# Graph layer on one core: eight segments instead of six, zero writes in equal steps, a staged tail, and a bias that ScalarE copies into PSUM

## Chip, cores and metric

The kernel runs on one core of one Trainium2 chip. The metric is the device time of one execution in microseconds, as the median of the runs. Five engines work side by side, each in the order of its own instructions: TensorE (PE, with its weight loads as PEld), VectorE (DVE), ScalarE (ACT), GpSimd (POOL) and SyncE (SP). SP, ACT and POOL issue the DMA transfers, and each of these queues is in order too.

## The reference

A SchNet-like graph layer with a residual. There are 12,500 nodes of 128 features and 412,500 edges, which come sorted by `dst`.

```python
def ssp(x):
    return jax.nn.softplus(x) - LOG2
hn = jnp.maximum(_layernorm(x, axis=-1), 0.0)
h = hn @ W_in2f                                               # 12500 x 128
Wij = ssp(edge_attr_20 @ W_f1 + b_f1) @ W_f2 + b_f2           # 412500 x 128
Wij = Wij * edge_weight[:, None]
agg = jax.ops.segment_sum(h[dst] * Wij, src, num_segments=12500)
out = x + ssp(agg @ W_o1 + b_o1) @ W_o2 + b_o2
```

So each edge reads the row of its `dst`, which lies close to the row of the edge before it, makes a message, and adds it to the row of its `src`, which lies anywhere.

## The kernel before

**Edges.** They are cut into 806 chunks of 512 edges (four tiles of 128), four chunks to a group, 202 groups. `step(k)` writes out by hand, for all engines, what is issued around chunk `k`, each piece of it for another chunk so that the pieces overlap: `hidden`, `hidden_log` and `hidden_end` make the softplus of the first layer for two chunks at a time (tiles `z`, `a`, `r`); `blocks`, `rank` and `rank_end` work out a free slot for every edge (`free` in PSUM, read by L660); `window`, `picked` and `value` make the two factors of the message; `message` multiplies them on DVE (L741, tile `o`, four buffers of two chunks) and issues four indirect DMAs on POOL (L745), one for each tile, which scatter the 128 rows into a table in HBM.

**The bias b_f2.** `value` (L723) opens the accumulation of a PSUM bank with a product of three rows of ones and three bf16 parts of the bias (L726), and adds the four products with `W_f2` to it (L730). `picked` (L709) makes the selected `h` rows in another bank (L714) and ACT copies them, scaled by the edge weight, into `hg` (L719). Both kinds of bank share the tag `v` with three buffers. The order in a step is product of chunk k (DVE), `value` of k+1, `picked` of k+1.

**Segments.** `SEGS` (L23) cuts the groups into six segments, each with its own slot table. A table gives every block of 128 nodes `T` tiles of 128 slots, and one more where the sorted `dst` of the segment bring the self loops; `T` follows from the segment's mean count and four standard deviations. When the last chunk of a segment is scattered, `Collect` reads the table back in units of up to six tiles: `load` (L783, SP queue, five buffers), `compare` (L794, DVE, a one-hot matrix of the place in the block), `add` (L807, two passes of TensorE for each tile). Four blocks, a quad, share one PSUM bank with a single buffer; when the quad is complete, `keep` adds it into `agg` (L824, DVE; the first segment's is an ACT copy, L822). Units are spread over later steps by a planner (L917 to L932) that gives each segment the smallest even rate of tiles with which all of it is done by step 812. In a step, `compare` comes after the message, `add` (one unit late) after the rank, and `rank_end` after `add`.

**Zero writes.** Slots that may stay empty must hold zeros. `clear` (L500) lists the DMA writes of a segment, each up to `ZN * ZR` = 32 slot rows for each of up to 128 half blocks, and L904 to L915 put them at steps: the first segment's before chunk 108, the second's in chunks 128 to 246, all others' in chunks 128 to 470. SP issues them at the start of a step. The first scatter past a given chunk of the first segment waits for that segment's writes.

**Tail.** After the loop the last segment is collected unit by unit (L970 to L977), and for each complete quad `finish` (L375) loads `x` (ACT queue), multiplies by `W_o1` (L389), does the softplus in four ACT instructions and one DVE sum (L366 to L373), multiplies by `W_o2` (L398), adds `b_o2` (L401) and the result (L402) to `x` on DVE, and stores (L403, SP queue). If a slot count was exceeded anywhere, a flag makes the kernel repeat the work in a plain loop (`anyway`).

Of the kernel before, what the change touches and what calls it, by code (L numbers as in the profile page):

```python
# [9 lines left out]
F32 = mybir.dt.float32  # L10
# [3 lines left out]
AF = mybir.ActivationFunctionType  # L14
ALU = mybir.AluOpType
PSUM = bass.MemoryType.PSUM

P = 128
TG = 16
CH = 512  # L20
NCHUNK = TG * P // CH
QT = CH // P
SEGS = (64, 56, 32, 24, 14, 12)  # L23
RW = P + 1
VIEWS = 16
BG = 8
ZR = 8
ZN = 4
WR = 32
UT = 6  # L30
BIG = float(1 << 11)
# [9 lines left out]
def gnn_kernel(  # L41
# [20 lines left out]
    nc = tc.nc  # L62
    N, D = x.shape
    NG, _, RBF, _ = f_t.shape
# [7 lines left out]
    const = ctx.enter_context(tc.tile_pool(name="const", bufs=1))  # L72

    NBLK = NTILE
# [52 lines left out]
    NQ = ceil_div(N, QN)  # L127
# [15 lines left out]
    state = ctx.enter_context(tc.tile_pool(name="state", bufs=1))  # L143
# [13 lines left out]
    for c0 in range(0, NC, P):  # L157
        n = min(P, NC - c0)
# [14 lines left out]
    for q in range(NQ):  # L173
        cs = slice(quad_of.index(q), quad_of.index(q) + quad_of.count(q))
# [29 lines left out]
    def spread(t, n):  # L204
        return t[:, None, :].to_broadcast([t.shape[0], n, P])
# [14 lines left out]
    flag = const.tile([1, 1], I32, name="flag")  # L220
# [9 lines left out]
    ones_b = const.tile([P, P], BF16, name="ones_b")  # L230
# [8 lines left out]
    nbf1 = const.tile([P, 1], F32, name="nbf1")  # L239
    nc.vector.tensor_scalar(nbf1, bf1, -1.0, None, op0=ALU.mult)  # L240

    bf2_p = const.tile([3, P], BF16, name="bf2_p")
    left = const.tile([1, P], F32, name="bf2_left")
    with tc.tile_pool(name="bias_ps", bufs=1, space=PSUM) as bias_ps:
        b12 = bias_ps.tile([1, P], F32, name="b12")
        nc.tensor.matmul(b12, bf1, wf2, start=True, stop=True)
        nc.vector.tensor_add(left, b12, bf2[0:1, :])
    for k in range(3):
        part = const.tile([1, P], BF16, name=f"bf2_{k}")
        nc.vector.tensor_copy(part, left)  # L250
# [117 lines left out]

    def softplus_end(a, r):

        nc.scalar.activation(a, a, AF.Exp, scale=-1.0)
        nc.scalar.activation(a, a, AF.Ln, bias=half, scale=0.5)
        nc.vector.tensor_add(r, r, a)  # L373

    def finish(t0, n, sT, edge, quad, psum):  # L375

        n0 = t0 * P
        full = min(n, N // P - t0)
        rest = N - n0 - full * P if full < n else 0
        xo = quad.tile([P, QT, P], F32, name="xo")  # L380
        pieces = []
        if full:
            pieces.append((P, slice(0, full), slice(n0, n0 + full * P)))
        if rest:
            pieces.append((rest, slice(full, n), slice(n0 + full * P, N)))
        for p, cs, rows in pieces:
            nc.scalar.dma_start(xo[:p, cs, :], x[rows, :].rearrange("(c p) f -> p c f", p=p))
        z = psum.tile([P, 2, CH], F32, name="z_out", tag="z")[:, 0, :n * P]
        nc.tensor.matmul(z, wo1, sT, start=True, stop=True)  # L389
        a = edge.tile([P, QT, P], F32, name="a_out")  # L390
        r = edge.tile([P, QT, P], F32, name="r_out")
        a_n = a[:, :n, :].rearrange("p c f -> p (c f)")
        r_n = r[:, :n, :].rearrange("p c f -> p (c f)")
        softplus_parts(a_n, r_n, z, bo1)
        softplus_end(a_n, r_n)
        v = psum.tile([P, QT, P], F32, name="v_out", tag="v", bufs=3)
        for i in range(n):
            nc.tensor.matmul(v[:, i, :], r[:, i, :], wo2, start=True, stop=True)  # L398
        for p, cs, rows in pieces:
            xi = xo[:p, cs, :]  # L400
            nc.vector.tensor_add(xi, xi, spread(bo2[:p, :], xi.shape[1]))  # L401
            nc.vector.tensor_add(xi, xi, v[:p, cs, :])  # L402
            nc.sync.dma_start(out[rows, :].rearrange("(c p) f -> p c f", p=p), xi)  # L403


    def anyway(edge, quad, psum):
        none = edge.tile([P, SUMT // parts * P], F32, name="none", bufs=1)
        nc.vector.memset(none, 0.0)
        rows = sums[:, :].rearrange("(p a c) f -> a p (c f)", p=P, a=parts)
# [3 lines left out]
        with tc.For_i(0, NG, 1) as g:  # L413
            f = edge.tile([P, CH], F32, name="f")
# [12 lines left out]
            a = edge.tile([P, NCHUNK, CH], F32, name="a")  # L427
            r = edge.tile([P, NCHUNK, CH], F32, name="r")
# [45 lines left out]
        for t0 in range(0, NTILE, QT):  # L474
            n = min(QT, NTILE - t0)
            o = quad.tile([P, QT, P], F32, name="s_out")
            nc.sync.dma_start(o[:, :n, :], sums[t0 * P:(t0 + n) * P, :].rearrange("(c p) f -> p c f", p=P))
            tps = psum.tile([P, QT, P], F32, name="t_out", tag="nodes")
            for i in range(n):
                nc.tensor.transpose(tps[:, i, :], o[:, i, :], ident)  # L480
            sT = quad.tile([P, QT, P], F32, name="sT")
            nc.scalar.activation(sT[:, :n, :], tps[:, :n, :], AF.Copy)
            finish(t0, n, sT[:, :n, :].rearrange("p c f -> p (c f)"), edge, quad, psum)


    with tc.tile_pool(name="edge", bufs=2) as edge, tc.tile_pool(
# [4 lines left out]
        kept = {}  # L491
# [40 lines left out]
        class Group:  # L532
# [170 lines left out]
            def window(self, c):  # L703

                at = quad.tile([WP, CH], BF16, name="at")
                nc.vector.tensor_tensor(at, self.rel[:, c, :], prow, op=ALU.is_equal)  # L706
                self.pick = at

            def picked(self, c, at):  # L709

                ps = psum.tile([P, QT, P], F32, name="picked", tag="v", bufs=3)
                near = self.near.pop(c)
                for i in range(QT):
                    nc.tensor.matmul(ps[:, i, :], at[:, i * P:(i + 1) * P], near,  # L714
                                     start=True, stop=True)
                hg = quad.tile([P, QT, P], F32, name="hg", bufs=2)
                for i in range(QT):
                    j = c * QT + i
                    nc.scalar.activation(hg[:, i, :], ps[:, i, :], AF.Copy,  # L719
                                         scale=self.rcut[:, j:j + 1])  # L720
                return hg

            def value(self, c):  # L723

                v = psum.tile([P, QT, P], F32, name="v", bufs=3)
                nc.tensor.matmul(v.rearrange("p t f -> p (t f)"), ones_b[:3, :], spread(bf2_p, QT),  # L726
                                 start=True, stop=False, skip_group_check=True)
                r = self.pair[c // 2 * 2][:, c % 2, :]
                for i in range(QT):
                    nc.tensor.matmul(v[:, i, :], r[:, i * P:(i + 1) * P], wf2,  # L730
                                     start=False, stop=True, skip_group_check=True)
                return v

            def message(self, c, v, hg):

# [95 lines left out]
        def of(k):  # L831
            return groups[k // NCHUNK], k % NCHUNK

        hgs, ats, vs = {}, {}, {}

        summed = []

        def step(k, units=()):
# [24 lines left out]
            if has(k + 2):  # L863
                g, c = of(k + 2)
                g.window(c)
                ats[k + 2] = g.pick
# [34 lines left out]
        collects = [Collect(seg) for seg in segs]  # L901
        AHEAD = 3

        seg = segs[0]  # L904
        todo = clear(seg)
        for i, d in enumerate(todo):
            zeros.setdefault(i * (seg.cleared - 20) // len(todo), []).append((seg, d))
        todo = clear(segs[1])
        for i, d in enumerate(todo):
            zeros.setdefault(seg.cleared + i * (seg.c1 - 10 - seg.cleared) // len(todo),  # L910
                             []).append((segs[1], d))
        todo = [(seg, d) for seg in segs[2:] for d in clear(seg)]
        for i, d in enumerate(todo):
            zeros.setdefault(segs[0].cleared + i * (segs[2].c0 - 10 - segs[0].cleared)
                             // len(todo), []).append(d)  # L915
# [33 lines left out]
        with tc.manual_schedule():  # L949
# [17 lines left out]
                step(k, now)  # L967
                next(aside, None)
            summed[0].add(summed[1])
        last = collects[-1]  # L970
        for u in range(len(last.units)):
            last.load(u)
            last.compare(u)
            last.add(u)
            for done in last.kept:
                finish(*done, edge, quad, psum)
            last.kept = []  # L977
        worst = state.tile([1, 1], F32, name="worst")
        nc.vector.tensor_reduce(worst, bad, axis=mybir.AxisListType.X, op=ALU.max)
        nc.vector.tensor_copy(flag, worst)  # L980

    missed = nc.values_load(flag[0:1, 0:1], min_val=0, max_val=P)
    with tc.If(missed > 0):
# [53 lines left out]
```

## Time and profile before

| | us |
|---|---|
| median of 3 runs | 4383.54 (4381.74 to 4402.45) |
| the profiled execution | 4396.31 |
| its span, first to last instruction | 4394.5 |
| first scatter starts | 85.1 |
| last scatter starts | 4220.6 |
| first compare of the last segment | 4234.8 |

The mean granted TensorE clock is 0.855. Over the span it goes from 0.64 to 0.72 in the stretches up to 1400 us, where hardly anything is collected, to 0.90 to 0.95 after it. The memory traffic is 829 MB, 189 GB/s on average. The zero writes are 164 DMAs of up to 2,064 KB, the table reads 829 of 193.5 to 387 KB.

In the groups of instructions a row gives the line, engine, operation, what is written from what, the count, busy time, mean ns of one, and the engine's idle time just before with what ended it. In the stretches a row gives start and end, length, the engine's busy time with its count, granted clock, DMA share and GB/s. A row of a timeline gives start, duration, engine, line and operation, and in brackets how long the engine was idle before and what released it.

### The profile page before, as it was taken

How to read it: one execution, taken by the hardware profiler on the slowest of the kernel's cores; microseconds unless marked ns; L12 is line 12 of the kernel's file. 1: busy time of each engine (PE TensorE's matmuls, PEld its weight loads, DVE VectorE, ACT ScalarE, POOL GpSimd, SP SyncE). 2: the span in 40 equal slices, each digit the busy share in tenths (PEclk: the TensorE clock that was granted, in tenths of full speed). 3: DMA queues.
4: the chain of work that ended last, by engine and by line, in shares of the span. 5: the costliest groups of instructions: out<-in, count | busy, mean ns of one | idle time of the engine just before them, and what ended most of it. 6: DMA issues, size and time to landing. Idle time of an engine off the chain costs nothing.

```text
span 4394.5 us, 72656 instructions
## 1 busy us (share of the span) xinstructions
PE 3607.4 (82%) x22558; PEld 2618.3 (60%) x22558; DVE 3140.1 (71%) x6637; ACT 2332.5 (53%) x4685; POOL 3114.6 (71%) x3288
## 2 busy tenths in 40 slices
PE   3767776777777888888788889999899998989877
PEld 2544444444444666666566567777677776767666
DVE  5766666566555776767667678787888878888766
ACT  3655555555555555555555555555555555545424
POOL 2777777677777777777777777777777777777620
PEclk9776666667666898899998899999999999999999
DMA  5766547888765666765876566666666766766666
GB/s 139 192 178 230 174 128 197 223 223 230 183 208 135 177 178 183 238 193 166 257 197 174 150 179 187 194 195 185 189 188 183 199 191 185 193 188 191 172 180 192
DMA packets 498071, 829.10 MB, mean 189 GB/s; under 512 B 170680, under 2 KB 288300, under 8 KB 497676
## 3 DMA queue, kind: packets, MB, share of 16 engines
q1 hardware_dynamic: 378950, 602.34, 51.2%
q0 software_dynamic: 103168, 213.15, 14.7%
q10 hardware_dynamic: 15558, 8.89, 0.7%
q8 instruction: 182, 2.98, 0.3%
q14 instruction: 213, 1.74, 0.1%
HBM read 425.03 MB, written 398.98 MB: 188 GB/s over the span
## 4 chain that ended last, share of the span: by engine, by line


## 5 line engine op out<-in xcount | busy, mean ns | idle before, releaser
L745 POOL DMA_INDIRECT slots<-o,slot x3224 | 3108.4, 964 | 1106.3 <-issue 803.6
L719 ACT ACTIVATE hg<-picked,rcut 128x128 f32<-128x128 f32 x3224 | 920.8, 369 | 1372.0 <-PE picked L714 1323.5
L807 PEld LDWEIGHTS acc<-to,m 128*128 128x128 f32 x8312 | 1078.7, 205 | 353.8 <-issue 187.7
L807 PE MATMUL acc<-to,m 128*128 128x128 f32 x8312 | 1154.6, 294 | 92.3 <-DVE agg L824 47.3
L730 PEld LDWEIGHTS v<-wf,r 128*128 128x128 f32 x6448 | 918.1, 220 | 303.7 <-issue 303.7
L730 PE MATMUL v<-wf,r 128*128 128x128 f32 x6448 | 1088.2, 320 | 0.0
L616 PE MATMUL z<-f,wf 20*128 20x512 f32 x1612 | 524.2, 726 | 217.5 <-DVE r L631 190.9
L794 DVE TENSOR_TENSOR to<-count_ps,m 128x768 f32<-128x768 f32 (+3 forms) x829 | 657.9, 812 | 51.8 <-PE acc L807 27.7
L619 ACT ACTIVATE a<-z,bf 128x1024 f32<-128x1024 f32 x403 | 449.1, 1114 | 426.7 <-PE z L616 426.7
L660 DVE TENSOR_REDUCE top<-free 128x4 f32<-128x392 f32 x806 | 447.2, 555 | 211.7 <-PE free L655 210.4
L631 DVE SCALAR_TENSOR_TENSOR r<-z,nbf,a 128x1024 f32<-128x1024 f32 x403 | 514.6, 1277 | 94.2 <-ACT a L625 92.5
L741 DVE TENSOR_TENSOR o<-v,hg 128x512 f32<-128x512 f32 x806 | 547.2, 679 | 2.8 <-ACT hg L719 2.1
L739 DVE COPY o<-place 128x8 f32<-128x8 f32 x403 | 80.4, 200 | 650.9 <-DMA slots<-o,slot 650.6
L714 PE MATMUL picked<-near,at 96*128 96x128 bf16 x3224 | 356.4, 240 | 218.0 <-DVE o L741 215.7
L625 ACT ACTIVATE a<-a,half 128x1024 f32<-128x1024 f32 x403 | 468.4, 1162 | 0.0
L636 DVE TENSOR_TENSOR inb<-count_ps,blk 128x392 f16<-128x392 f32 x806 | 445.7, 553 | 0.0
L726 PE MATMUL v<-bf_p,ones_b 3*128 3x512 bf16 x806 | 350.1, 434 | 104.1 <-DVE o L741 93.9
L620 ACT ACTIVATE a<-a 128x1024 f32<-128x1024 f32 x403 | 425.9, 1057 | 12.8
L714 PEld LDWEIGHTS <-at 96*128 96x128 bf16 x3224 | 275.7, 109 | 256.2 <-DVE o L741 224.6
L616 PEld LDWEIGHTS z<-f,wf 20*128 20x128 f32 x1612 | 142.4, 206 | 388.9 <-issue 186.3
L687 PE MATMUL free<-inb,rest_of 128*128 128x392 f16 x806 | 303.1, 376 | 55.0 <-DVE top L660 53.8
L706 DVE TENSOR_TENSOR at<-rel,prow 96x512 bf16<-96x512 bf16 x806 | 331.1, 411 | 0.0
(107 smaller groups left out, 1416.2 us busy)
## 6 DMA issues: line engine op xcount, KB each, us to landing
m<-slots SPq DMA_DIRECT2D x371, 387.0 KB
rel<-rel_d SPq DMA_DIRECT2D x202, 384.0 KB
m<-slots SPq DMA_DIRECT2D x172, 322.5 KB
m<-slots SPq DMA_DIRECT2D x212, 258.0 KB
slots<-o,slot POOLq DMA_INDIRECT x3224
slots<-zero SPq DMA_DIRECT2D x24, 2064.0 KB
f<-in_f_t SPq DMA_DIRECT2D x404, 80.0 KB
slots<-zero SPq DMA_DIRECT2D x22, 1032.0 KB
```

The lines of the kernel that those rows point to most:

```text
L616: nc.tensor.matmul(z[:, k, :], wf1[rows, :], self.f[rows, :], start=True, stop=True)
L619: nc.scalar.activation(a, z, AF.Abs, bias=bf1)
L625: nc.scalar.activation(a, a, AF.Ln, bias=half, scale=0.5)
L631: nc.vector.scalar_tensor_tensor(r, z, nbf1, a, op0=ALU.max, op1=ALU.add)
L660: nc.vector.tensor_reduce(self.top[:, c * QT:(c + 1) * QT], free_v, axis=mybir.AxisListType.X, op=ALU.max)
L714: nc.tensor.matmul(ps[:, i, :], at[:, i * P:(i + 1) * P], near, start=True, stop=True)
L719: nc.scalar.activation(hg[:, i, :], ps[:, i, :], AF.Copy, scale=self.rcut[:, j:j + 1])
L730: nc.tensor.matmul(v[:, i, :], r[:, i * P:(i + 1) * P], wf2, start=False, stop=True, skip_group_check=True)
L741: nc.vector.tensor_mul(o[:, :, :P], v, hg)
L745: put = nc.gpsimd.indirect_dma_start(out=views[j % VIEWS], out_offset=bass.IndirectOffsetOnAxis(ap=self.slot[:, j:j + 1], axis=0), in_=o[: ...
L794: nc.vector.tensor_tensor(to[:, :n, :], count_ps[:, None, :].to_broadcast([P, n, P]), self.m[u][:, :n, P:].to_broadcast([P, n, P]), op=ALU ...
L807: nc.tensor.matmul(self.acc[b // QT][:, i, :], m[:, j, :P], to[:, j, :], start=t == 0, stop=t == self.seg.tiles(b) - 1)
```

## The change

- `SEGS` becomes eight segments of 68, 52, 30, 14, 14, 8, 8 and 8 groups.
- `ZN` becomes 1, so that a zero write covers 8 slot rows of a half block instead of 32. All segments' writes go through one rule that gives each segment a due step and spreads the writes evenly up to it.
- `value` splits: `bias` fills the bank two chunks ahead, for chunks 0 and 1 with the product as before, for all others with an ACT copy of `bf12` (the bias on all partitions); `value` adds the four products to it. `picked` splits into `pick` (the four products, now one accumulation group of the bank) and `picked` (the four ACT copies). ACT's order in a step is the bias of k+2, then the copies of k+1.
- `bf12` is made in the preamble by a product with 128 columns instead of one.
- The tail comes into the hand-written order. `finish` becomes a generator of six stages, which are issued for different quads around each `add`: load of `x` (now SP), `b_o2` on POOL, first product and softplus on ACT, sum on DVE, second product, result and store. `xo` has six buffers; `a_out` and `r_out` share the loop's tiles. The flag is worked out ahead of the tail.

```diff
-SEGS = (64, 56, 32, 24, 14, 12)
+SEGS = (68, 52, 30, 14, 14, 8, 8, 8)
...
-ZN = 4
+ZN = 1
...
-        b12 = bias_ps.tile([1, P], F32, name="b12")
-        nc.tensor.matmul(b12, bf1, wf2, start=True, stop=True)
-        nc.vector.tensor_add(left, b12, bf2[0:1, :])
+        b12 = bias_ps.tile([P, P], F32, name="b12")
+        nc.tensor.matmul(b12, bf1.to_broadcast([P, P]), wf2, start=True, stop=True)
+        nc.vector.tensor_add(bf12, b12, bf2)
+    nc.vector.tensor_copy(left, bf12[0:1, :])
...
-    def finish(t0, n, sT, edge, quad, psum):
+    def finish(t0, n, sT, quad, psum):
...
-        xo = quad.tile([P, QT, P], F32, name="xo")
+        xo = quad.tile([P, QT, P], F32, name="xo", bufs=6)
...
-            nc.scalar.dma_start(xo[:p, cs, :], x[rows, :].rearrange("(c p) f -> p c f", p=p))
+            nc.sync.dma_start(xo[:p, cs, :], x[rows, :].rearrange("(c p) f -> p c f", p=p))
+        yield
+        for p, cs, rows in pieces:
+            xi = xo[:p, cs, :]
+            nc.gpsimd.tensor_add(xi, xi, spread(bo2[:p, :], xi.shape[1]))
+        yield
...
         softplus_parts(a_n, r_n, z, bo1)
-        softplus_end(a_n, r_n)
+        softplus_logs(a_n)
+        yield
+        nc.vector.tensor_add(r_n, r_n, a_n)
+        yield
...
+            nc.tensor.matmul(v[:, i, :], r_n[:, i * P:(i + 1) * P], wo2, start=True, stop=True)
+        yield
         for p, cs, rows in pieces:
             xi = xo[:p, cs, :]
-            nc.vector.tensor_add(xi, xi, spread(bo2[:p, :], xi.shape[1]))
             nc.vector.tensor_add(xi, xi, v[:p, cs, :])
...
+            def bias(self, c):
+
+
+                v = psum.tile([P, QT, P], F32, name="v", bufs=3)
+                if self.g * NCHUNK + c < 2:
+                    nc.tensor.matmul(v.rearrange("p t f -> p (t f)"), ones_b[:3, :],
+                                     spread(bf2_p, QT), start=True, stop=False,
+                                     skip_group_check=True)
+                else:
+                    nc.scalar.activation(v, spread(bf12, QT), AF.Copy)
+                return v
...
             if has(k + 1):
                 g, c = of(k + 1)
-                vs[k + 1] = g.value(c)
+                vs[k + 1] = g.value(c, bs.pop(k + 1))
+                ps = psum.tile([P, QT, P], F32, name="picked", tag="v", bufs=3)
+                g.pick(c, ats.pop(k + 1), ps)
+            if has(k + 2):
+
+                bs[k + 2] = of(k + 2)[0].bias(of(k + 2)[1])
             if has(k + 1):
-                g, c = of(k + 1)
-                hgs[k + 1] = g.picked(c, ats.pop(k + 1))
+                hgs[k + 1] = g.picked(c, ps)
...
+        clears = [(seg, d) for seg in segs for d in clear(seg)]
+        due = [seg.cleared - 20 if seg is segs[0] else seg.c0 - 10 for seg in segs]
+        todo = [sum(seg is s for s, _ in clears) for seg in segs]
+        t0, i = 0, 0
+        while i < len(segs):
+
+            j = max(range(i, len(segs)), key=lambda j: sum(todo[i:j + 1]) / (due[j] - t0))
+            n = sum(todo[i:j + 1])
+            for m in range(n):
+                zeros.setdefault(t0 + m * (due[j] - t0) // n, []).append(clears.pop(0))
+            t0, i = due[j], j + 1
...
+            go(0)
+            go(1)
+            for u in range(AHEAD):
+                last.load(u)
+            go(0)
+            last.compare(0)
+            q = 0
+            for u in range(len(last.units)):
+                last.load(u + AHEAD)
+                if u + 1 < len(last.units):
+                    last.compare(u + 1)
+                if last.kept:
+                    last.kept = []
+                    go(q - 4)
+                last.add(u)
+                if last.kept:
+                    go(q + 2)
+                    go(q + 1)
+                    go(q - 1)
+                    go(q - 2)
+                    go(q - 3)
+                    q += 1
```

`go(q)` advances quad `q` by one stage.

More of the change, by code (lines that the diff above doesn't have):

```diff
@@ L240, in gnn_kernel @@
     nc.vector.tensor_scalar(nbf1, bf1, -1.0, None, op0=ALU.mult)
+    bf12 = const.tile([P, P], F32, name="bf12")
     bf2_p = const.tile([3, P], BF16, name="bf2_p")
@@ L369, in softplus_end, with softplus_logs @@
     def softplus_end(a, r):
+        softplus_logs(a)
+        nc.vector.tensor_add(r, r, a)
+    def softplus_logs(a):
         nc.scalar.activation(a, a, AF.Exp, scale=-1.0)
         nc.scalar.activation(a, a, AF.Ln, bias=half, scale=0.5)
-        nc.vector.tensor_add(r, r, a)
-    def finish(t0, n, sT, edge, quad, psum):
+    def finish(t0, n, sT, quad, psum):
         n0 = t0 * P
@@ L386, in finish @@
         for p, cs, rows in pieces:
-            nc.scalar.dma_start(xo[:p, cs, :], x[rows, :].rearrange("(c p) f -> p c f", p=p))
+            nc.sync.dma_start(xo[:p, cs, :], x[rows, :].rearrange("(c p) f -> p c f", p=p))
[4 more added lines that the diff above has]
+        yield
         z = psum.tile([P, 2, CH], F32, name="z_out", tag="z")[:, 0, :n * P]
         nc.tensor.matmul(z, wo1, sT, start=True, stop=True)
[L390 to L393, printed above, removed]
+        a_n = quad.tile([P, 2, CH], F32, name="a_out", tag="a", bufs=2)[:, 0, :n * P]
+        r_n = quad.tile([P, 2, CH], F32, name="r_out", tag="r", bufs=3)[:, 0, :n * P]
         softplus_parts(a_n, r_n, z, bo1)
-        softplus_end(a_n, r_n)
+        softplus_logs(a_n)
+        yield
+        nc.vector.tensor_add(r_n, r_n, a_n)
+        yield
         v = psum.tile([P, QT, P], F32, name="v_out", tag="v", bufs=3)
         for i in range(n):
-            nc.tensor.matmul(v[:, i, :], r[:, i, :], wo2, start=True, stop=True)
+            nc.tensor.matmul(v[:, i, :], r_n[:, i * P:(i + 1) * P], wo2, start=True, stop=True)
+        yield
         for p, cs, rows in pieces:
             xi = xo[:p, cs, :]
-            nc.vector.tensor_add(xi, xi, spread(bo2[:p, :], xi.shape[1]))
             nc.vector.tensor_add(xi, xi, v[:p, cs, :])
@@ L482, in anyway @@
             nc.scalar.activation(sT[:, :n, :], tps[:, :n, :], AF.Copy)
-            finish(t0, n, sT[:, :n, :].rearrange("p c f -> p (c f)"), edge, quad, psum)
+            for _ in finish(t0, n, sT[:, :n, :].rearrange("p c f -> p (c f)"), quad, psum):
+                pass
     with tc.tile_pool(name="edge", bufs=2) as edge, tc.tile_pool(
@@ L706, in window, with value, pick @@
                 nc.vector.tensor_tensor(at, self.rel[:, c, :], prow, op=ALU.is_equal)
-                self.pick = at
-            def picked(self, c, at):
-                ps = psum.tile([P, QT, P], F32, name="picked", tag="v", bufs=3)
+                self.at_w = at
+            def bias(self, c):
[7 more added lines that the diff above has]
+                return v
+            def value(self, c, v):
+                r = self.pair[c // 2 * 2][:, c % 2, :]
+                for i in range(QT):
+                    nc.tensor.matmul(v[:, i, :], r[:, i * P:(i + 1) * P], wf2,
+                                     start=False, stop=True, skip_group_check=True)
+                return v
+            def pick(self, c, at, ps):
                 near = self.near.pop(c)
@@ L714, in picked @@
                     nc.tensor.matmul(ps[:, i, :], at[:, i * P:(i + 1) * P], near,
-                                     start=True, stop=True)
+                                     start=i == 0, stop=i == QT - 1, skip_group_check=True)
+            def picked(self, c, ps):
                 hg = quad.tile([P, QT, P], F32, name="hg", bufs=2)
@@ L721, in picked @@
                 return hg
[L723 to L732, printed above, removed]
             def message(self, c, v, hg):
@@ L832, in of @@
             return groups[k // NCHUNK], k % NCHUNK
-        hgs, ats, vs = {}, {}, {}
+        hgs, ats, vs, bs = {}, {}, {}, {}
         summed = []
@@ L865, in step @@
                 g.window(c)
-                ats[k + 2] = g.pick
+                ats[k + 2] = g.at_w
             if has(k):
@@ L902, in gnn_kernel @@
         AHEAD = 3
[L904 to L915, printed above, removed]
+        clears = [(seg, d) for seg in segs for d in clear(seg)]
[8 more added lines that the diff above has]
+            t0, i = due[j], j + 1
         at = [seg.c1 + 9 for seg in segs[:-1]]
@@ L969, in gnn_kernel, with go @@
             summed[0].add(summed[1])
[L970 to L980, printed above, removed]
+            worst = state.tile([1, 1], F32, name="worst")
+            nc.vector.tensor_reduce(worst, bad, axis=mybir.AxisListType.X, op=ALU.max)
+            nc.vector.tensor_copy(flag, worst)
+            last = collects[-1]
+            outs = []
+            for b in range(0, NBLK, QT):
+                n = min(QT, NBLK - b)
+                sT = kept["agg"][:, b:b + n, :].rearrange("p c f -> p (c f)")
+                outs.append(finish(b, n, sT, quad, psum))
+            def go(q):
+                if 0 <= q < NQ:
+                    next(outs[q], None)
+            go(0)
[20 more added lines that the diff above has]
+                    q += 1
+            for q in range(NQ, NQ + 5):
+                go(q - 4)
+                go(q - 1)
+                go(q - 2)
+                go(q - 3)
     missed = nc.values_load(flag[0:1, 0:1], min_val=0, max_val=P)
```

## The prediction, made before the changed kernel was run

> **What bounds the kernel now.** I read the page's busy table and costliest groups first, then the busy time of the scatter line in seven stretches, then the products that feed it with their counts, then the timeline of the tail.
>
> ```profile
> PE 3607.4 (82%) x22558; PEld 2618.3 (60%) x22558; DVE 3140.1 (71%) x6637; ACT 2332.5 (53%) x4685; POOL 3114.6 (71%) x3288
> ...
> L745 POOL DMA_INDIRECT slots<-o,slot x3224 | 3108.4, 964 | 1106.3 <-issue 803.6
> L719 ACT ACTIVATE hg<-picked,rcut 128x128 f32<-128x128 f32 x3224 | 920.8, 369 | 1372.0 <-PE picked L714 1323.5
> ```
>
> TensorE looks busiest, but POOL's row matters: 964 ns of work for each of 3,224 scatters, and most of its idle time is "issue", about 0.3 us of POOL's own between two. Per stretch (start:end, length, POOL busy and scatters, clock, DMA share, GB/s):
>
> ```profile
> 120.00:660.00 540.00, 409.81 (x425) 0.72 0.61 179
> 660.00:1100.00 440.00, 313.21 (x325) 0.67 0.81 218
> ...
> 1400.00:2600.00 1200.00, 911.81 (x946) 0.90 0.66 189
> 2600.00:3800.00 1200.00, 911.56 (x947) 0.95 0.68 191
> ...
> 4100.00:4222.00 122.00, 81.61 (x85) 0.90 0.56 154
> ```
>
> From 1400 to 3800 a scatter goes out every 2400/1893 = 1.268 us: POOL sets the pace, 5.07 us for a chunk of four, and nothing removed from another engine there shortens it. In 660:1100 there are 325 scatters where 440/1.268 = 347 fit: 28 us lost. The waits of that stretch put POOL behind its own earlier scatters' landing, at the highest DMA share of the table. In 4100:4222 there are 85 for 96: 14 us lost, and there POOL waits for DVE's product. First scatter at 85.1, last start at 4220.6; 3224 x 1.268 = 4088, so an unhindered end is 4173, and 47 us are lost, 42 of them in these two places.
>
> Why POOL starves at the end: DVE's products (L741) with the collecting adds (L824) in two stretches.
>
> ```profile
> L741 DVE TENSOR_TENSOR o<-v,hg x53: 672/677/681, 3661.8 to 3924.4; 128x512 f32<-128x512 f32 x53
> 3662.00:3928.00 266.00, 14.15 (x21) 0.97 0.71 198
> ```
> ```profile
> L741 DVE TENSOR_TENSOR o<-v,hg x26: 673/678/690, 4072.4 to 4213.2; 128x512 f32<-128x512 f32 x26
> 4072.00:4214.00 142.00, 11.67 (x17) 0.92 0.57 157
> ```
>
> With 21 adds on 53 chunks (0.40 each) the producing chain makes a chunk in 262.6/52 = 5.05 us. With 17 on 26 (0.65 each, the segment with three tiles a block) it takes 140.8/25 = 5.63, slower than POOL. An add holds one TensorE bank and sits in DVE's order ahead of rank, blocks and r, and z on TensorE waits for r: a handshake, not load.
>
> The rest is the tail. The last segment's first compare starts at 4234.8, 13 us after POOL's end (4221.6); the span ends at 4394.5, so collecting and the last layers take 159.7. One quad of it:
>
> ```profile
> 4250.86 0.97 PEld L398 LDWEIGHTS v_out<-wo,r_out 128*128 128x128 f32 x8 [0.86 <-DVE r_out L373]
> 4250.86 1.16 PE L398 MATMUL v_out<-wo,r_out 128*128 128x128 f32 x8 [0.68 <-DVE r_out L373]
> ...
> 4251.86 1.02 PE L389 MATMUL z_out<-agg,wo 128*128 128x512 f32 x2
> ...
> 4252.72 2.84 PE L807 MATMUL acc<-to,m 128*128 128x128 f32 x24
> ```
>
> TensorE goes round v, z, twelve tiles, with a wait for the softplus sum: 5.37 us from agg to agg (4245.36 to 4250.73), more when x or bo2's sum is late.
>
> **The change, part by part.** The base is the profiled span, 4394.5 (execution 4396.3, 12.8 above the median 4383.5 of the runs); what I sum is a difference and is taken from the median.
>
> Preamble: b_f2's product has 128 columns instead of one and one copy more. L730's 320 ns for two passes against L246's 394 for one column, plus one 0.2 us copy: 0 to +0.5, taken +0.4, in case it reaches the first scatter.
>
> Even clearing: 164 zero writes (147 MB by the segment formulas, up to 2,064 KB each) become 636 (158 MB, at most 516 KB), spread over chunks 0 to 766. The formulas put 47.6 MB on chunks 113 to 200 before, which at 5.07 us is the stretch 660:1100; now no 87 chunks get over 27. Chunks 0 to 113 had 33 MB before with 425 scatters in 540 us, a pace of 1.271. So the 28 us should come back. Against it, 43 MB now fall after chunk 489, where there were none. At the bad stretch's price (28 us for 47.6 MB) that is +25 at worst; at the price of chunks 0 to 113, nothing. I take -28 and 0, the density being the lower one. The 472 extra issues cost SP 0.45 us each (median of the zero writes), 212 us spread over 3,900, ahead of loads that are issued three units or six chunks early: nothing, and up to 0.45 a step without that lead.
>
> Bias: 804 products of 434 ns leave TensorE (349 us) and 804 copies of 128x512 enter ScalarE, by L822's 583 ns about 469 us, from 53% to 64% busy. While POOL sets the pace both are worth nothing; the cover is the products' lead over POOL, without which up to 0.58 a chunk would show. The copy waits for a PSUM bank, freed at worst by DVE's product of chunk k; behind it queue the four copies of chunk k+1 and the logarithm, for which DVE's product and r wait. Their cover is ScalarE's 1372 us of idle before L719, 1.7 us a chunk. In the late chain the bias product ran while TensorE was ahead of DVE in steps with an add, so I credit 0.15 of its 0.43 us (ends 0 and 0.43).
>
> The Trainium skill speaks against this part: "TensorE: Matmul & The Clock Gate", Part 1, says that the array's clock is halved after a window of about 3.4 us without enough work. The trace agrees that such slowing happens late: 24 products at 4136.1 took 2.90 us, 24 at 4153.3 took 5.49. By that rule the removed work would be paid back as slower products and the credit would be 0, which moves the sum by 0.15 x 120 = 18 us.
>
> Segments: two more, with 14, 14, 8, 8, 8 groups at the end. Tiles in all hardly move (4156 to 4180), but each segment has 25 adds. By the planner's rule the segments of three tiles are collected in chunks 686 to 761 (75 chunks, 0.67 adds each) and those of two in 761 to 806 (45 chunks, about one add each). For 0.67 the row is 5.63; less 0.15 it is 5.48 (ends 5.07 and 5.8). For one add a chunk the trace has no stretch. From below, it is no faster than 5.63 - 0.43 = 5.2; from above, the slope (5.63 - 5.05)/(0.65 - 0.40) = 2.3 us per add gives 5.63 + 0.35 x 2.3 = 6.4. I take 5.85, near the middle since eight-tile steps are even. Lateness: 75 x 0.41 = 31, 45 x 0.78 = 35, and one more segment end in this part (3.1 us of DVE from 3933.2 to 3936.3 in the timeline, products at half speed after it; I put it at 8): 74. Until about 3200 the products start some 25 us before their scatters (four buffers of two chunks); that lead goes first, so POOL loses about 49 where it lost 14: +35.
>
> Tail: b_o2's sum goes to POOL, x's load to SP and six buffers, z, softplus and v one quad apart, two tiles a block. POOL's 25 adds of 128x512 stand behind the scatters; DVE's row (L401) says 659 ns, the affine_select of 128x128 (282 ns) four times 1.1 us; either hides under a quad, and each is needed three quads later. A quad: 5.37 less eight matmul records of 0.118 is 4.42; less the wait of 0.68 it is 3.75; by DMA, about 1.04 MB at the tail's 215 GB/s is 4.8. I take 4.4: 22 quads 97, two of three tiles 10.7, the half quad 3, lead-out 11 (10 from the last agg now): 122 against 159.7, -38 (ends -20 and -50).
>
> Sum: 0.4 - 28 + 35 - 38 = **-30.6**: span 4364, median **4353**.
>
> **Rivals.** (1) The late chain keeps up: without the bias product late chunks stay near 5.2 and the lead covers most. For it: 5.05 at 0.40 adds. Against: 5.63 at 0.65. POOL then loses 8, six less than now: 0.4 - 28 - 6 - 38 = -72, 4312. (2) The adds decide, the slower side: at 0.67 and one add a chunk on chunks 686 to 806 every step pays the handshake and the halved clock, 5.79 (the products from 4072.4 to 4176.6: 104.2/18) and 6.9. Lost: 75 x 0.72 + 45 x 1.83 + 8 - 25 = 119, 105 over now; with 0.4 - 28 - 38 that is +39: 4423. It decides from about 6.1 at one add a chunk with 5.79 before it. (3) The clearing is paid back late: forecast plus 25, 4378. For it: loads of 258 KB give three units less cover. Against: 27 MB per 87 chunks cost nothing early. (4) It does not do what it says: the smaller segments overflow and the fallback runs, milliseconds; their limits lie four to five standard deviations out.
>
> **How the numbers follow.** Forecast 0.49, (1) 0.28, (2) 0.14, (3) 0.08, (4) 0.01. Likeliest 4353. Its own bounds are the late chain (49, from 10 to 90) and the tail (-20 to -50): 4302 to 4412 with both at one end. 8 in 10: 4298, which takes in (1), to 4402, which leaves out (2). A measurement of this kernel tells about 0.5% (22 us) from no change: faster is 4361.6 or less, which takes most of the forecast, all of (1) and a little of (3): 0.66. Same 0.18, slower 0.16 with (2), (4) and the forecast's upper end.
>
> **What would show it.** 660:1100 with about 347 scatters shows the clearing right. The last scatter starts near 4175 if (1), near 4220 if the forecast, beyond 4260 if (2). L741's pitch over the last 45 chunks is the figure that decides: 5.85 expected. In the tail, agg to agg 4.4 us, and about 135 from POOL's end to the span's; more than 150 would mean that DMA or a wait replaced the one removed. The forecast is wrong if the products lose no lead before chunk 760, or if POOL waits for landings after chunk 489.

## The result and the profile after

The changed kernel takes 4419.71 us (median of 7 runs, 4416.1 to 4432.82) against 4385.03 for the kernel before: a ratio of 1.0085, 95% interval 1.0072 to 1.0097. It is 35 us slower where 30 less were forecast, and lies outside the range. The profiled execution has a span of 4416.9, 22.4 over that of before.

The page after, the busy table and two groups:

```profile
PE 3425.1 (78%) x21802; PEld 2670.5 (60%) x21802; DVE 3193.9 (72%) x6745; ACT 2681.7 (61%) x5489; POOL 3181.6 (72%) x3314
...
L770 POOL DMA_INDIRECT slots<-o,slot x3224 | 3144.0, 975 | 1131.1 <-issue 805.5
...
L732 ACT ACTIVATE v<-bf 128x512 f32<-128x512 f32 x804 | 478.0, 595 | 1497.3 <-DVE o L766 1496.6
```

350 us of bias products left TensorE, but its busy time fell by 182 only: its other products ran longer (the collecting ones 304 ns instead of 294, those of `value` 329 instead of 320). The copies that came for them (L732) are 478 us where 469 was estimated, and they wait 1497 us for DVE's product, which nobody minds as long as POOL sets the pace. But the scatter has a mean of 975 ns instead of 964, on a line that the change did not touch. The scatter's own line (min/median/max, first and last start), after and then before:

```profile
L770 POOL DMA_INDIRECT slots<-o,slot x3224: 962/968/1782, 80.3 to 4280.9; - x190
```
```profile
L745 POOL DMA_INDIRECT slots<-o,slot x3224: 952/958/1438, 85.1 to 4220.6; - x190
```

The minimum and the median both move by 10 ns: every scatter got longer, not a few. The stretches of after (length, POOL busy and scatters, clock, DMA share, GB/s):

```profile
660.00:1100.00 440.00, 335.71 (x343) 0.67 0.55 159
...
1400.00:2600.00 1200.00, 914.02 (x939) 0.85 0.67 199
...
3800.00:4100.00 300.00, 198.45 (x205) 0.89 0.62 178
```

In 660:1100 there are 343 scatters instead of 325 and the DMA share fell from 0.81 to 0.55. In 1400:2600 there are 939 instead of 946: a pace of 1.278 us instead of 1.268. In 3800:4100 there are 205 where 300/1.278 = 235 fit: POOL starves. The last scatter starts 60.3 us later than before.

And the collecting adds of the tail, of after (`keep` is now L849):

```profile
L849 DVE TENSOR_TENSOR agg<-agg,acc x28: 421/677/689, 4286.7 to 4403.7; 128x512 f32<-128x512 f32 x26, 128x256 f32<-128x256 f32 x2
```

28 adds in 117 us are 4.33 us a quad, and from the last scatter's start to the span's end it is 136 us, against 174 before. Span against span, by the prediction's terms:

| | predicted | measured | from |
|---|---|---|---|
| start | +0.4 | -5 | first scatter 85.1 to 80.3 |
| clearing | -28 | -23 | 18 more scatters in 660:1100, at 1.278 |
| every scatter | 0 | +26 | 9.5 ns x some 2,700 at POOL's own pace |
| late chain | +35 | +62 | the rest of the 60.3 |
| tail | -38 | -38 | 174 to 136 |
| sum | -30.6 | +22 | |

The medians are 35 apart and not 22, since the profiled execution of before was one of its longer ones.

### The profile page after: what moved, and what is told of

It reads as the page before. It is cut to its first block, busy times and chain, and to the rows that moved or that the text cites. A ratio compares the mean times of both kernels' runs of the same rounds, so it can differ in the third digit from the quotient of the medians.

```text
span 4416.9 us, 72344 instructions
## 1 busy us (share of the span) xinstructions
PE 3425.1 (78%) x21802; PEld 2670.5 (60%) x21802; DVE 3193.9 (72%) x6745; ACT 2681.7 (61%) x5489; POOL 3181.6 (72%) x3314
## 4 chain that ended last, share of the span: by engine, by line
## 5 line engine op out<-in xcount | busy, mean ns | idle before, releaser
L770 POOL DMA_INDIRECT slots<-o,slot x3224 | 3144.0, 975 | 1131.1 <-issue 805.5
L832 PEld LDWEIGHTS acc<-to,m 128*128 128x128 f32 x8360 | 1141.0, 214 | 445.2 <-issue 183.3
L732 ACT ACTIVATE v<-bf 128x512 f32<-128x512 f32 x804 | 478.0, 595 | 1497.3 <-DVE o L766 1496.6
L739 PE MATMUL v<-wf,r 128*128 128x128 f32 x6448 | 1118.0, 329 | 332.3 <-ACT v L732 331.4
L832 PE MATMUL acc<-to,m 128*128 128x128 f32 x8360 | 1236.9, 304 | 172.7 <-DVE to L819 73.5
L739 PEld LDWEIGHTS v<-wf,r 128*128 128x128 f32 x6448 | 1000.6, 237 | 567.0 <-ACT v L732 560.1
L819 DVE TENSOR_TENSOR to<-count_ps,m 128x640 f32<-128x640 f32 (+3 forms) x873 | 662.2, 783 | 54.4 <-DMA m<-slots 43.4
L747 PE MATMUL picked<-near,at 96*128 96x128 bf16 x3224 | 372.5, 247 | 0.0
L747 PEld LDWEIGHTS <-at 96*128 96x128 bf16 x3224 | 301.2, 114 | 30.3
L669 PE MATMUL free<-inb,after 128*128 128x392 f16 x806 | 309.9, 384 | 5.6 <-DVE inb L650 2.9
```

The lines of the kernel that those rows point to most:

```text
L732: nc.scalar.activation(v, spread(bf12, QT), AF.Copy)
L739: nc.tensor.matmul(v[:, i, :], r[:, i * P:(i + 1) * P], wf2, start=False, stop=True, skip_group_check=True)
L770: put = nc.gpsimd.indirect_dma_start(out=views[j % VIEWS], out_offset=bass.IndirectOffsetOnAxis(ap=self.slot[:, j:j + 1], axis=0), in_=o[: ...
L819: nc.vector.tensor_tensor(to[:, :n, :], count_ps[:, None, :].to_broadcast([P, n, P]), self.m[u][:, :n, P:].to_broadcast([P, n, P]), op=ALU ...
L832: nc.tensor.matmul(self.acc[b // QT][:, i, :], m[:, j, :P], to[:, j, :], start=t == 0, stop=t == self.seg.tiles(b) - 1)
```

## Experiments

e5 to e8, e13 to e16, e17 and e18 ran where a clock of 0.72 to 0.75 was granted and the kernel before takes 5812 to 5885; they are compared among themselves. All others ran at 0.82 to 0.86, with the kernel before at 4390 or 4391. In kernels made from the one before, the scatter is L745, L757 or L758. More than the clock differs in the first group. e5 and e10 are the same kernel; the shortest and the median of `value`'s products are 269 and 275 ns in e5, 270 and 275 in e10. But e5 has waits that end on nothing the profile names, and e10 has none of them, such as this one (total, times, longest):

```profile
DVE top L674 <- remote: 909.7, 131, 12.6
```

So the lower mean clock can be a result of these waits, and what holds the kernel there is not shown.

**Each part alone, on the kernel before.** e1: the segments.

```diff
-SEGS = (64, 56, 32, 24, 14, 12)
+SEGS = (68, 52, 30, 14, 14, 8, 8, 8)
```

> The kernel before with the eight segments alone. Theory (the adds set the late pace): with 0.67 and about one add a chunk the products run at 5.6 to 5.9 us a chunk from chunk 686 on, POOL loses 45 to 80 us there where it lost 14, the tail is about 20 us shorter with eight tiles a quad: 4385 + 10 to + 45, 4395 to 4430. Rival (the ScalarE copy of the bias makes the lateness, the adds alone do not): the products stay near 5.3, POOL loses under 25 us, and the time is 4360 to 4375.

e2: `ZN = 1` and the even schedule of zero writes.

> The kernel before with the finer, even zero writes alone. Theory (they give back 23 to 28 us between 660 and 1100 us and cost nothing else): 4357 to 4362, scatters of 964 ns on average as before. Rival (the finer zero writes are what lengthened every scatter from 964 to 975 ns in the changed kernel, 32 us over 3224): 4385 - 25 + 32, about 4390, with a median scatter of 968 ns instead of 958.

e3: `bf12`, `bias`, `pick` and the new order of `value`, bias and `picked`.

> The kernel before with the ScalarE copy of the bias alone. Theory (the copy waits for DVE's product of chunk k and holds the copies of chunk k+1 and the logarithm behind it, so the chain of DVE, ScalarE and TensorE becomes slower per chunk): the pace of the products without POOL's limit grows from 5.2 to 5.4 or more from chunk 600 on, POOL starves earlier and loses 40 us or more: 4410 to 4440. Rival (the copy is hidden and relieves TensorE): late pace at or under 5.1, no loss at the end, 4370 to 4385. If this part lengthens every scatter, its median is 968 ns instead of 958 and 32 us come on top.

e4: the generator `finish` and the staged loop behind the last chunk, with x's load on SP and b_o2's sum on POOL.

> The kernel before with the staged tail alone (twelve tiles a quad stay). Theory: a quad goes from about 6.0 to 5.2 us, the time from POOL's end to the span's end from 173 to about 155: 4365 to 4372. Rival (the tail's gain in the changed kernel, 173 to 135, comes from the eight tiles a quad alone): no change, 4380 to 4390.

| | median us | ratio (95%) | scatter median ns | last scatter | to the span's end |
|---|---|---|---|---|---|
| e1 segments | 4427.81 | 1.0078 (1.0061 to 1.0095) | 958 | 4280.7 | 148 |
| e2 clearing | 4377.88 | 0.9972 (0.9961 to 0.9983) | 958 | 4204.0 | 172 |
| e3 bias | 4387.09 | 0.9997 (0.9983 to 1.0011) | 958 | 4208.1 | 174 |
| e4 tail | 4398.27 | 1.0015 (1.0005 to 1.0025) | 967 | 4234.1 | 166 |

The four differences, +34, -12, -1 and +7 (each ratio times 4391), make about +27 of the 35. e2 gives back less than its theory said, e3 lies near its rival, and e4 is slower than both of its forecasts. Three readings. The segments alone lose as much as the whole change. Most of the tail's gain is theirs too: 26 of the 38 us come with two-tile blocks in the old serial tail (174 to 148), and the staging alone brings 8. And it is the tail's edit that lengthens the scatters, though its instructions run after the last of them: 9.5 ns on each of 3224 are up to 31 us. In e4 the last scatter starts 13.5 us later than before, which outweighs the 8 gained behind it. Why the staging brings little, from the waits behind the last scatter, in e4 and then before (total, times, longest):

```profile
DVE to L806 <- DMA m<-slots: 43.2, 40, 4.1
```
```profile
DVE to L794 <- DMA m<-slots: 6.9, 7, 2.3
L824 DVE TENSOR_TENSOR agg<-agg,acc x29: 410/679/687, 4222.2 to 4384.5; 128x512 f32<-128x512 f32 x27, 128x256 f32<-128x256 f32 x2
```

In the staged tail the compares wait for the tables' loads, as they hardly did before. e9 below, staged and with three tiles a block, has 28 adds from 4205.3 to 4350.0, 5.36 us a quad; the old tail's 29 adds (second line of before) are 5.79 apart. So the staging takes 0.4 us off a quad, and the loads take over.

**What lengthens the scatters.** e5 is the changed kernel, e6 the kernel before, e7 the changed one with the six old segments, e8 as e7:

```diff
e5, e8:
-            nc.gpsimd.tensor_add(xi, xi, spread(bo2[:p, :], xi.shape[1]))
+            nc.vector.tensor_add(xi, xi, spread(bo2[:p, :], xi.shape[1]))
e6:
-            nc.vector.tensor_add(xi, xi, spread(bo2[:p, :], xi.shape[1]))
+            nc.gpsimd.tensor_add(xi, xi, spread(bo2[:p, :], xi.shape[1]))
```

> The changed kernel whole, with only the sum of b_o2 and x on VectorE again. The staged tail alone lengthened every scatter's issue on POOL (median 967 ns against 958). Theory A: the 26 POOL adds of b_o2 are the cause, by being in POOL's program: median 958 here, so about 3224 x 10 ns = 32 us less, about 4390. Theory B: the cause is something else of the staged tail (x loads on SP, six xo buffers and so other addresses, the flag's place): median 967 to 968, and the time stays at 4415 to 4425.

> The kernel before, with only the sum of b_o2 and x put on POOL, in the old serial tail. Theory A (the POOL add's presence lengthens the scatters): median 967 to 968 instead of 958, first to last, though every add runs after the last scatter; the time then +30 for the scatters and up to 26 x 0.55 = 14 for the adds' own length, about 4415 to 4435. Theory B: median 958 and 4385 to 4405.

> The changed kernel with the six old segments (64, 56, 32, 24, 14, 12). If the parts add up: 4391 - 12 (clearing) - 1 (bias) + 6 (tail, POOL adds and all) = about 4384, scatter median 968, last scatter near 4235 and 150 behind it. If the eight segments are needed for the staged tail or the parts hinder one another: 4400 or more.

> The six old segments, even clearing, the bias copy and the staged tail, with b_o2's sum on VectorE. Theory A: scatter median 958, 4384 - 32 = about 4352, faster than the kernel before by about 0.9%. Theory B: as e7, about 4384.

e5 and e8 have 958, e7 has 967, so it goes with POOL's adds. But e6 has the same 26 adds behind the scatters of the old tail, and

```profile
L745 POOL DMA_INDIRECT slots<-o,slot x3224: 952/958/1629, 84.1 to 5703.2; - x190
```

so the adds alone are not enough. The times: e5 1.0081 (1.0056 to 1.0107), e6 0.9967 (0.9941 to 0.9993), e7 0.9922 (0.9894 to 0.9951), e8 0.9945 (0.9926 to 0.9964). On these chips the 10 ns cost nothing, e7 is not behind e8: POOL is not the bound there. The scatter's group on e5's page:

```profile
L770 POOL DMA_INDIRECT slots<-o,slot x3224 | 3106.3, 964 | 2668.5 <-DVE o L766 1758.7
```

It sits idle 2668 us, most of it until DVE's product, where after had 1131. The segments, however, cost 1.4% here too (e5 against e8).

So e8 and e5 ran once more where the clock is higher, as e9 and e10, with two probes beside them. e12 is e7 with a second `nc.gpsimd.memset(zero, 0.0)` ahead of all scatters; e11 comes below.

> The six old segments, even clearing, the bias copy, the staged tail and b_o2's sum on VectorE, on another chip than e8's (there the kernel before took 5885 and the granted clock was 0.73). By the parts measured at a clock of 0.85: kernel before - 12 (clearing) - 1 (bias) + 6 (tail with POOL adds) - 32 (scatters at 958 ns instead of 967) = 39 less, a ratio of 0.991. If the scatters' 10 ns were hidden behind the chunks: 7 less, 0.998.

> The changed kernel with b_o2's sum on VectorE, on the same chip as e9. If the whole +35 of the changed kernel is eight segments (+34) and lengthened scatters (+32) against clearing, bias and tail: 35 - 32 = +3, a ratio of 1.000 to 1.002. If in the late chain, where the chunks decide and not POOL, shorter scatters bring nothing: about 30 x 2800/3224 = 27 less, +8, 1.002. If the segments alone decide: 1.008 as before.

> The changed kernel with the six old segments and b_o2's sum on POOL (scatters of 967 ns), and one memset more on POOL ahead of all scatters, which writes the same zeros again. Theory A (the adds on POOL in the staged tail lengthen the scatters, wherever the program lies): median 967 again. Theory B (where POOL's instructions come to lie decides, and the 26 adds only move that): another median, 958.

e9: 4357.57, 0.9924 (0.9901 to 0.9948); e10: 4404.25, 1.0031 (1.0014 to 1.0048). Both have 958 ns. e12 has 967 still, so moving POOL's program by one instruction is not it; its one execution took 4388.8, 31 more than e9, which is 3224 x 9.5 ns. Against after's 1.0085, e10 gets back 0.5%, 24 us. Two more probes are e9 with one POOL add (`nc.gpsimd if t0 == 0 else nc.vector`) and e9 with a POOL memset of a spare tile beside each of DVE's sums:

> The six old segments and the rest as in e9 (scatters of 958 ns), but the first quad's sum of b_o2 on POOL, 25 on VectorE. Theory A (one add on POOL in the staged tail is enough to lengthen all scatters): median 967. Theory B (it takes many): 958.

> As e9, b_o2's sum on VectorE, and a memset of a spare tile on POOL beside each sum, so as many POOL instructions in the tail as the changed kernel's adds. Theory A (any work of POOL behind the scatters lengthens them): median 967. Theory B (it is the two-operand add): 958.

```profile
L771 POOL DMA_INDIRECT slots<-o,slot x3224: 962/967/1637, 84.1 to 5636.6; - x190
```
```profile
L772 POOL DMA_INDIRECT slots<-o,slot x3224: 956/962/1633, 82.3 to 5641.5; - x190
```

One add (first line, e15) does what 26 do. With 26 memsets (second, e16) the median is 962, which neither theory foresaw. But e13 and e17, below, are one kernel without any POOL work in the tail, run on two chips, and they differ as much:

```profile
L770 POOL DMA_INDIRECT slots<-o,slot x3224: 952/958/1772, 82.7 to 5703.7; - x190
```
```profile
L770 POOL DMA_INDIRECT slots<-o,slot x3224: 956/962/1632, 82.6 to 5683.0; - x190
```

So 4 ns can come without any edit, and e16 does not show that the memsets do it. Shown: all five kernels with one or 26 POOL adds in the staged tail have a median of 967 or 968, whatever the segments, the clearing or the bias; of the 14 traces with no POOL work there, 13 have 958 and e17 has 962. Not settled: why e6's adds do nothing, and what moves e17. No trace shows how work at the end of POOL's program reaches instructions that ran before it.

**What the late chain pays.** e11 is e1 with the collecting add shrunk:

```diff
-                        nc.vector.tensor_add(sums_b, sums_b, acc[:, :b + 1 - b0, :])
+                        w = 8 if self.seg in segs[2:-1] else P
+                        nc.vector.tensor_add(sums_b[:, :, :w], sums_b[:, :, :w],
+                                             acc[:, :b + 1 - b0, :w])
```

> The kernel before with the eight segments alone (4428, +34), but VectorE's add of a quad's sums into agg shrunk from 512 to 32 columns for the third to the seventh segment, so most of those sums are left out: about 125 adds x 0.6 us = 75 us less of VectorE between chunks 600 and 806, the same instructions, products and waits. Theory A (VectorE's time in the late chain is the price): the late chunks go from 5.8 to about 5.4 us, the last scatter comes at about 4230 instead of 4281 and the time at 4380 to 4395. Theory B (the price is the handshakes between PE, VectorE and SP for more and smaller units, and the products run at a halved clock): the chunks stay at 5.7 to 5.8 us and the time within 10 of 4428.

It took 4368.42, 0.9949 (0.9934 to 0.9964), against e1's 1.0078: theory A, and more than it asked for. The adds and DVE's products between chunks 686 and 761, in e1:

```profile
L824 DVE TENSOR_TENSOR agg<-agg,acc x50: 420/688/690, 3599.5 to 4016.5; 128x512 f32<-128x512 f32 x48, 128x256 f32<-128x256 f32 x2
```
```profile
L741 DVE TENSOR_TENSOR o<-v,hg x76: 672/678/680, 3596.0 to 4018.4; 128x512 f32<-128x512 f32 x76
```

and in e11:

```profile
L825 DVE TENSOR_TENSOR agg<-agg,acc x50: 170/188/189, 3585.4 to 3976.9; 128x32 f32<-128x32 f32 x48, 128x16 f32<-128x16 f32 x2
```
```profile
L741 DVE TENSOR_TENSOR o<-v,hg x76: 673/678/682, 3583.0 to 3978.3; 128x512 f32<-128x512 f32 x76
```

Fifty adds in 75 chunks, each 0.50 us shorter, are 0.33 us of DVE a chunk; the chunk falls from 422.4/75 = 5.63 us to 395.3/75 = 5.27, by 0.36. The same adds, products and banks are there, and so is DVE's wait at the add for TensorE's sums, in e1 and in e11 (total, times, longest):

```profile
DVE agg L824 <- PE acc L807: 75.7, 40, 5.2
```
```profile
DVE agg L825 <- PE acc L807: 71.3, 40, 3.2
```

So the length of an add on DVE counts one for one. What the waits around it cost is not shown to be nothing: they remain, and 5.27 us is still more than POOL's 5.07. Between before and e1 a chunk has 0.31 adds more (27 and 50 in 75 chunks) and is 0.35 us longer: 1.1 us an add with all that comes with it, where the add itself lasts 0.69.

The same reading for the others (clock in 3600:3780):

| | 686 to 761, us a chunk | 761 to 805 | lead at 686 | clock |
|---|---|---|---|---|
| before | 5.28 | 5.38 | 17.6 | 0.94 |
| e1 segments | 5.63 | 5.74 | 14.9 | 0.95 |
| e3 bias | 5.13 | 5.39 | 16.1 | 0.91 |
| e9 old segments, all else | 5.15 | 5.64 | 11.4 | 0.94 |
| e12 as e9, sum on POOL | 5.19 | 5.48 | 6.2 | 0.91 |
| after | 5.95 | 5.54 | 13.3 | 0.82 |
| e10 after, DVE sum | 6.08 | 5.74 | 14.4 | 0.80 |

The lead is the time from a chunk's product to its first scatter. Alone, the bias copy makes the chunks from 686 to 761 shorter by 0.15 us, and with clearing and tail beside it and the old segments (e9, e12) they stay there. With eight segments around it they are 0.3 to 0.45 us longer than e1's, at a lower clock. e9 and e12, which differ among the late chunks only in the scatters' 9 ns, are 0.04 and 0.16 apart. The windows of e1 and of after (PE, PEld, DVE, ACT and POOL busy, clock, DMA share, GB/s):

```profile
3600.00:3780.00 180.00, 156.61 (x1103) 121.58 (x1104) 146.59 (x288) 88.92 (x180) 134.77 (x141) 0.95 0.66 179
```
```profile
3600.00:3780.00 180.00, 146.95 (x925) 120.19 (x922) 128.57 (x255) 93.77 (x189) 122.85 (x127) 0.82 0.68 203
```

TensorE, DVE and POOL do less in after, and ScalarE, which has the copies, 4.9 us more; none is full: they wait for one another. Two of the waits in that window of after, and four instructions (start, length):

```profile
ACT v L732 <- DVE o L766: 77.1, 27, 7.8
DVE agg L849 <- PE acc L832: 38.4, 17, 4.2
```
```profile
3690.11 1.91 PE L739 MATMUL v<-wf,r 128*128 128x128 f32 x8
...
3694.27 0.60 ACT L732 ACTIVATE v<-bf 128x512 f32<-128x512 f32 x1 [2.19 <-DVE o L766]
...
3696.62 1.60 PE L832 MATMUL acc<-to,m 128*128 128x128 f32 x12 [2.19 <-DVE agg L849]
...
3698.22 1.05 PE L739 MATMUL v<-wf,r 128*128 128x128 f32 x8
```

Eight products of `value` take 1.91 us in one step and 1.05 in the next. ScalarE's copy starts only after DVE's product, and TensorE stands 2.19 us until DVE's add frees the one `acc` bank: a round through DVE, in which TensorE has gaps. These rows do not show which gap lowers the clock: the fast eight come right after the 2.19 us. The tables' loads are not most of it: between chunks 686 and 761 DVE's compares wait 4.9 us for them in after and 1.7 in e1, while the 75 chunks take 24 us more.

e13 and e17 are e10 with e11's edit:

> The changed kernel with b_o2's sum on VectorE and, as in e11, VectorE's adds into agg shrunk from 512 to 32 columns for the third to the seventh segment, so most of those sums are left out. Theory A (what remains of the loss is VectorE's time in the late chain): the 56 us that e11 gained come off here too: 1.003 - 0.013 = a ratio of 0.990, last scatter near 4220, within 10 of the six old segments (0.992). Theory B (in the whole change it is the bias copy on ScalarE and its waits for VectorE's product that hold the late chain, and the adds less): 0.998 to 1.003.

> e13's kernel again, hoped to run where the granted clock is 0.82 to 0.85 and the kernel before takes about 4390 (e13 ran at 0.73: before 5812, ratio 1.000, against 1.008 of the same kernel with full adds). The changed kernel with b_o2's sum on VectorE and the adds of the third to the seventh segment shrunk to 32 columns, most of those sums left out. Theory A (VectorE's time in the late chain is what remains of the loss): 0.990, last scatter near 4220, within 10 of e9's 0.992. Theory B (the bias copy's waits hold the late chain more than the adds): 0.998 to 1.003.

Both fell on the slower clock: 1.0003 (0.9976 to 1.0031) and 0.9998 (0.9977 to 1.0019), against e5's 1.0081. That is within theory B's figures, but these were meant for the higher clock. On the slower chips the adds' time is worth some 47 us of the whole change, rather more than half of what parts e5 from e8. At the higher clock this was not run, and neither was the changed kernel with the old bias product, or the eight segments with the bias copy alone. That the bias copy is what lowers the clock in after is therefore inferred, from e3, e9, e10 and e12, and not shown.

**A small last segment with fewer segments.** e14 and e18 are e8 with `SEGS = (66, 56, 34, 24, 14, 8)`:

> Six segments (66, 56, 34, 24, 14, 8) with even clearing, the bias copy, the staged tail and b_o2's sum on VectorE. Against e9 (64, 56, 32, 24, 14, 12; 0.992) the work behind the last scatter falls from 165 to 137 us, and the fifth segment of three-tile blocks is collected over the last 21 chunks instead of 37. If the late chain does not lose more than e9's: 4357 - 28 = 4330, a ratio of 0.986. If those 21 chunks go from 6.3 to 7.5 us and more: 0.992 or worse.

> e14's kernel again (e14 ran at a clock of 0.73: ratio 0.9956): six segments (66, 56, 34, 24, 14, 8), even clearing, the bias copy, the staged tail, b_o2's sum on VectorE. If the late chain loses no more than e9's: 28 less than e9, a ratio of 0.986. If the last 21 chunks, which collect 310 tiles instead of 37 chunks, go from 6.3 to 7.5 us: the same as e9, 0.992; beyond that, worse.

0.9956 (0.9928 to 0.9985) and 0.9947 (0.9916 to 0.9978), the same as e8's 0.9945 at that clock: no gain there; at the higher clock it stays open.

The best version run is **e9**, 0.9924: the change with the old segments and b_o2's sum on VectorE, faster than both kernels.

## Why the prediction was wrong

- **The bound, right.** POOL set the pace to chunk 680 or so, the products' lead went first, and the end was decided in the last 120 chunks.
- **Scatter's pace, missed.** The step said of POOL's 25 adds that they "stand behind the scatters" and hide under a quad. They do hide: their median is 1.27 us at 4.33 us a quad. The step put them at nothing; with them in the staged tail each of 3224 scatters takes 10 ns more, 24 to 31 us (e10 against after, e12 against e9). No row of before could have shown it; the range had nothing for it, and how it comes about stays open.
- **Late chain, mis-sized: 75 chunks at 5.48, measured 5.95.** The row of 5.63 was right: e1, with the bias product in place, has 5.63. The step that failed is "less 0.15": the removed product was taken for a gain, with an end of 0 at worst. With the six old segments the gain is there (e3: 5.28 to 5.13); in the whole change the chunks are 0.32 longer than e1's. That is 75 x 0.47 = +35. What makes them longer when copy and eight segments meet stays open. One add a chunk was put at 5.85 and measured 5.54: 44 x 0.31 = -14. A lead of 25 was credited where 13 were left: +12. And 8 for a segment's end were counted apart that the pitch already holds: -8. Together +25, of the 27 in the table.
- **"A handshake, not load", wrong about the load.** e11 takes only length from the adds, and the last scatter starts at 4220.7, where before has 4220.6. The waits remain, so their price is open. The slope of 2.3 us an add was too steep: before against e1 gives 1.1, and e1's own two stretches, 0.67 and 1.00 adds at 5.63 and 5.74, give 0.3.
- **The clock.** In 3600:3780 the granted clock is 0.82 in after against e1's 0.95, and eight products of `value` take 1.91 or 1.05 us; TensorE's longest wait for r there is 4.2 us in after and 3.3 in e1. The Trainium skill ("TensorE: Matmul & The Clock Gate", Part 1) says that the array's clock is halved after an idle window of about 3.4 us. The rows agree with that direction. The prediction priced it as paying back 18 us. The rival that rested on it, at 4423, came nearest, in part by luck: its 5.79 measured 5.95, but its 6.9 measured 5.54, and the scatters' 26 us, which it did not have, made up for that.
- **Clearing, right in place, worth half in the end.** 343 scatters where 347 were expected. Of the 28 us a part is given back where the lead runs out (e2: last scatter 16.6 earlier, 12 by the ratio); POOL's waits for landings after 2560 us are 0.3 us at the longest.
- **Tail, right sum, wrong reason.** 4.33 us a quad against 4.4, 135 from POOL's end. But the 5.37 it started from was one of the faster quads (5.79 on average), and e1 and e4 show that two tiles a block bring 26 of the 38 us; the staging brings 8 alone and 12 on top of e1. With three tiles the compares wait for the tables' loads.
- **Bias copy, covered where it was said to be.** e3's 0.9997: its copies wait 1448 us for DVE's product, which costs nothing while POOL sets the pace. The term that failed is the late one above.

## What to carry to other kernels

Where one engine's lead over the bound is all the slack there is, price each extra instruction of the late stretch at no less than its length on the engine that the chain runs through, and test that by shrinking the instruction and leaving the waits. A credit for removed work that holds in one arrangement can turn into a loss in another, as here with six and eight segments: let its range go below zero. And after moving work to the engine that sets the pace, compare the duration of one unchanged instruction of it, also where the moved work runs last.

## What was not expected of the hardware

- An indirect DMA's issue on POOL took 952, 956 or 962 ns at the least and a median of 6 more, one figure for the 3224 of a run. The 962 came in the five kernels with POOL adds in the staged tail and in no other, where the granted clock was 0.73 and where it was 0.83; one kernel, run twice, had 952 and 956.
- POOL's add of 128x512 took a median of 1.27 us against 0.69 of DVE's (L401 before). The Trainium skill ("GPSIMD Engine Reference", section 4.1) has GpSimd about two times slower for elementwise operations with two inputs. The rows agree: 1.27/0.69 is 1.8.
- On chips where the mean granted clock was 0.73 the same kernel took 5812 to 5885 us instead of 4390. The products' shortest and median lengths were the same there; the waits that end on nothing named were new.
